# Two quarters of an edge chunk in one set of score columns: a graph-attention kernel, its first layer changed

## The chip, the cores and the metric

The kernel runs on one core of a Trainium2 chip. The metric is the device time of one execution in microseconds (us). The kernel before takes 2269.68 us, the median of three runs (2267.27 to 2270.17).

## What is computed

Two graph-attention layers over 6,250 nodes of 128 features and 106,250 directed edges, which arrive sorted by their destination (`dst`). Each edge carries 64 message features and 32 cosine features of a time difference. Each of two heads scores an edge, the scores are turned into weights by a softmax over the edges that end in one node, and the weighted values are summed per node. Between the layers stand a batch normalisation and a relu, and behind the second layer a residual and a layer norm.

```python
q = (h @ Wq + bq).reshape(n, H, C)
k = (h @ Wk + bk).reshape(n, H, C)
v = (h @ Wv + bv).reshape(n, H, C)
e = (edge_attr @ We).reshape(-1, H, C)
alpha = einsum('ehc,ehc->eh', q[dst], k[src] + e) / sqrt(C)
a = segment_softmax(alpha, dst)
out = segment_sum((v[src] + e) * a[:, :, None], dst) + h @ Ws + bs
```

All arithmetic is in 32-bit floats.

## The kernel before

**Chunks.** A preparation cuts the sorted edges into `NC` = 105 chunks. A chunk owns at most `NN` = 64 consecutive nodes and loads a window of `CE` = 1024 edges (`T` = 8 tiles of 128). A node and a head make one score row, so a chunk has 64 x 2 = 128 rows. The preparation also tests whether the edges are sorted and whether the cuts fit; it adds up what is wrong (`worst`, `bad`, `tot`) and writes a flag `oki` (L1521 to L1526). With the flag set `ordered` runs, otherwise a slower general path.

**One chunk in layer 1** (`conv(0)`). `gather` (L796) has GpSimd fetch the source node's row for 128 edges with one indirect DMA, so eight per chunk, into tile `ff`. `transfers` (L740) sends the chunk's stores and loads on SyncE's queue: two held stores, the message rows (`fedge`, one DMA of 256 KB) and the table `ftab`, which holds for each of the 128 score rows the vector that an edge is multiplied with. `encode` (L820) makes the cosine features on VectorE (DVE) and ScalarE (ACT). `turn_in` (L849) transposes features into `fft` and `fet` (edges along the free axis). `score` (L879) makes, for each half of the chunk, a 128 x 512 tile `fps` of scores with two matmuls (L887 for node features, L888 for edge features and for a code: where an edge doesn't belong to the row's node, the code adds 2^120). `lowest` (L890) takes each row's minimum, `weigh` (L898) the exponential of the negated score, which is zero where the code was added. `turn_weights` (L904) transposes the 128 x 1024 weights in eight steps into `fpt`, with edges along the partitions, and `gather_sums` (L917) adds weights times features in eight matmuls of 225 columns (L921) into `fpa`. `divide`, `finish_turn`, `apply` and `finish` make the node's output of it.

**Order.** The instructions of each engine run in the order in which the code is written. A round k of the loop at L1125 works on several chunks at once: scores of chunk k, sums of chunk k-1, output of chunk k-2, `turn_in` of chunk k+1, `encode` of chunk k+2 and gathers of chunk k+3. The gathers are paced: `tick` (L812) ties the next gather to a step of TensorE (PE) in the round, eight in a round of layer 1. Some rounds take on other work (`rest`, L1232): the tables of later nodes (L630) and, behind them, rows of the result. The last two chunks of a layer are written out by hand (`first_ends`, L1039). Layer 2 (`conv(1)`) has the same stages with edge data that layer 1 stored, and gathers eight tiles at a time without pacing (`fetch_whole`, L807).

**Weights in two passes.** A 32-bit matmul of the program appears in the profile as two MATMUL instructions, each with a weight load (LDWEIGHTS); a transpose appears as one.

Of the kernel before, what the change touches and what calls it, by code (L numbers as in the profile page):

```python
# [7 lines left out]
F32 = mybir.dt.float32  # L8
I32 = mybir.dt.int32
AF = mybir.ActivationFunctionType  # L10
OP = mybir.AluOpType
AX = mybir.AxisListType

P = 128
D = 128
H = 2
C = D // H
# [5 lines left out]
GE = GT * P  # L23
# [21 lines left out]
T = 8  # L45
# [8 lines left out]
FW = 1 + D + EC  # L54

APART = 2.0 ** 120
HIGHEST = 2.0 ** 119

LG = 10
# [604 lines left out]
def ordered(ctx: ExitStack, tc: tile.TileContext, pl, x, dst, edge_attr_64, conv2, bn_g, bn_b, out):  # L664
# [39 lines left out]
    def conv(c, extra, first_blocks=None):  # L704
# [20 lines left out]
        ends = []  # L725

        done = []

        def send(to, ap, after=None):
            dma = nc.sync.dma_start(to, ap)  # L730
# [9 lines left out]
        def transfers(k, after=None):  # L740
            for to, ap in held:
                send(to, ap, after)
                after = None
            held.clear()
            if not on(k):
                return
            s = plan(k)
            lo, hi = first(k)
            if k % LOT == 0:
                n = min(LOT, NC - k)  # L750
                lot[:] = [nc.sync.alloc_register(name=f"at{c}_{k}_{i}") for i in range(2 * n)]
                nc.sync.load(lot, pl.starts[0:1, 2 * k:2 * (k + n)])
            s.nb = nc.sync.snap(lot[2 * (k % LOT)], min_val=lo, max_val=hi)
            s.edge = load.tile([P, T * (MSG + TD)], F32, name="fedge", bufs=4)
            s.msg = s.edge[:, :T * MSG].rearrange("p (t d) -> p t d", d=MSG)
            s.z = s.edge[:, T * MSG:].rearrange("p (t d) -> p t d", d=TD)
            if c:
                send(s.edge, edge_d[k], after)
            else:
                sl = nc.sync.snap(lot[2 * (k % LOT) + 1], min_val=0, max_val=E - CE)  # L760
                send(s.msg, edge_attr_64[bass.ds(sl, CE), :].rearrange("(p t) d -> p t d", t=T), after)
            s.tab = load.tile([P, NN * H, 3 - c], F32, name="ftab")
            nc.sync.dma_start(s.tab, pl.tab_d[c][:, bass.ds(s.nb, NN)].rearrange("p n h w -> p (n h) w"))
            if c:
                s.et = ets[k % len(ets)]
                nc.sync.dma_start(s.et, et_d[k])
                s.r = load.tile([NN, D], F32, name="fr", bufs=AHEAD + 3)
                nc.sync.dma_start(s.r, res_d[bass.ds(s.nb, NN), :] if k < NC - 1 else res_d[N - NN:N, :])
# [110 lines left out]
        def score(k, u):  # L879

            s = ch[k]
            if u == 0:
                s.ps = []
            ps = p_s.tile([P, GE], F32, name="fps")
            s.ps.append(ps)
            w = slice(u * GE, (u + 1) * GE)
            tick(nc.tensor.matmul(ps, s.tab[:, :, 0], s.ft[:, w], start=True, stop=False))  # L887
            tick(nc.tensor.matmul(ps, s.tab[:EC, :, 1], s.et[:, w], start=False, stop=True), True)  # L888
# [8 lines left out]

        def weigh(k):  # L898
            s = ch[k]
            s.s = work.tile([P, CE], F32, name="fs")  # L900
            for u in range(2):
                nc.scalar.activation(s.s[:, u * GE:(u + 1) * GE], s.ps[u], AF.Exp, bias=s.bias, scale=-1.0)  # L902

        def turn_weights(k):  # L904

            s = ch[k]
            s.pt = work.tile([P, CE], F32, name="fpt")
            for u in range(2):
                pp = p_tr.tile([P, GE], F32, name="fppt", tag="tr")
                for t in range(4):  # L910
                    at = u * GE + t * P
                    turn = nc.tensor.transpose(pp[:, t * P:(t + 1) * P], s.s[:, at:at + P], ident)  # L912
                tick(turn, u == 1)
                last = nc.scalar.copy(s.pt[:, u * GE:(u + 1) * GE], pp)  # L914
            return last

        def gather_sums(k, between=None):  # L917
            s = ch[k]
            s.pa = p_a.tile([P, D + EW], F32, name="fpa")
            for t in range(T):  # L920
                add = nc.tensor.matmul(s.pa, s.pt[:, t * P:(t + 1) * P], s.f[:, t, 1:1 + D + EW], start=t == 0,  # L921
                                       stop=t == T - 1)
                if t in (1, 4, 7):
                    tick(add)
                if between and t == T // 2 - 1:
                    between()
# [401 lines left out]
def tile_gnn_resnorm(ctx: ExitStack, tc: tile.TileContext, x, src, dst, edge_attr_64, edge_weight, node_vec,  # L1328
# [13 lines left out]
    with tc.tile_pool(name="plan", bufs=1) as pl, tc.tile_pool(name="planw", bufs=2) as mw, \  # L1342
# [134 lines left out]
        def columns(t, to):  # L1477
            if t.dtype != F32:
                f = mw.tile([NC, T, P], F32, name="rowf")
                nc.vector.tensor_copy(f, t[:NC])  # L1480
                t = f
            t = t.rearrange("c t p -> c (t p)").rearrange("c (p t) -> c t p", t=T)
            for t0 in range(0, T, 4):
                pt = pp.tile([P, 4, NC], F32, name="fpx")
                for i in range(4):
                    nc.tensor.transpose(pt[:, i], t[:NC, t0 + i], ident[:NC, :NC])
                nc.vector.tensor_copy(to[:, t0:t0 + 4], pt)

        for _ in matrices(nc, got, 0, keep, bank, pl):
# [28 lines left out]
        got.tw = broadcast(nc, keep, "ftw", time_w, TD)  # L1518
        got.tb = broadcast(nc, keep, "ftb", time_b, TD)
        nc.sync.dma_start(got.wv[0], conv1["Wv"])  # L1520
        pb = pp.tile([1, 1], F32, name="pb", tag="one", bufs=1)  # L1521
        nc.tensor.matmul(pb, worst, ones[:, 0:1], start=True, stop=True)
        nc.vector.tensor_copy(bad[:, 1:2], pb)
# [43 lines left out]
```

## Time and profile before

| what | value |
|---|---|
| median of three runs | 2269.68 us |
| the profiled execution's own time | 2270.48 us |
| its span, first to last instruction | 2268.6 us |
| granted TensorE clock, mean | 0.986 |
| instructions | 38241 |
| first gather of layer 1 starts | 40.13 us |
| last gather of layer 1 starts | 1133.88 us |
| first gather of layer 2 starts | 1171.41 us |

A row of the timeline reads: start, how long the piece lasts, engine, line, operation, output <- input, shapes, count, and in brackets how long the engine had been idle and what ended that. A row of the windows reads: stretch, its length, then for each engine its busy time and, in brackets, its instructions, then the granted TensorE clock, the share of the DMA engines and GB/s. "PEld" is TensorE's weight load, "POOL" is GpSimd, "SPq" a DMA that SyncE issues. A matmul's recorded end is modelled, so the pitch of TensorE's work is read from start to start.

### The profile page before, as it was taken

How to read it: one execution, taken by the hardware profiler on the slowest of the kernel's cores; microseconds unless marked ns; L12 is line 12 of the kernel's file. 1: busy time of each engine (PE TensorE's matmuls, PEld its weight loads, DVE VectorE, ACT ScalarE, POOL GpSimd, SP SyncE). 2: the span in 40 equal slices, each digit the busy share in tenths (PEclk: the TensorE clock that was granted, in tenths of full speed). 3: DMA queues.
4: the chain of work that ended last, by engine and by line, in shares of the span. 5: the costliest groups of instructions: out<-in, count | busy, mean ns of one | idle time of the engine just before them, and what ended most of it. 6: DMA issues, size and time to landing. Idle time of an engine off the chain costs nothing.

```text
span 2268.6 us, 38241 instructions
## 1 busy us (share of the span) xinstructions
PE 2187.3 (96%) x11482; PEld 1693.3 (75%) x11482; DVE 1333.6 (59%) x4147; ACT 1349.7 (59%) x2234; POOL 1615.0 (71%) x1701
## 2 busy tenths in 40 slices
PE   5899999999999999999979999999999999999997
PEld 3688887887888878888866777777777777776775
DVE  6577777777777777777745444444444444444443
ACT  3677777777777877777743444444444444444444
POOL 3777777777777777777726777777777777777773
PEclk8999999999999999999988999999999999999999
DMA  7666666666666666666638666666666666655552
GB/s 233 182 203 180 205 209 199 184 195 198 209 192 185 209 199 212 184 201 197 187 124 227 182 186 174 173 188 181 184 181 161 192 187 175 182 169 148 164 160 57
DMA packets 208864, 417.35 MB, mean 184 GB/s; under 512 B 45216, under 2 KB 113116, under 8 KB 205324
## 3 DMA queue, kind: packets, MB, share of 16 engines
q1 hardware_dynamic: 135930, 261.60, 37.2%
q0 software_dynamic: 54144, 112.01, 20.2%
q10 hardware_dynamic: 18578, 41.21, 5.0%
q8 instruction: 97, 1.59, 0.3%
q14 instruction: 115, 0.94, 0.1%
HBM read 274.63 MB, written 140.01 MB: 183 GB/s over the span
## 4 chain that ended last, share of the span: by engine, by line
PE 84%; POOL 6%; issue 4%; DMA 3%; DVE 2%; ACT 0%; SPq 0%; DVEq 0%; ACTq 0%; POOLq 0%
PE fpa L921 25%; PE fps L887 15%; PE fps L888 14%; PE fpx L860 7%; PE fppt L912 7%; POOL ff L796 6%; PE fpg L630 4%; PE fpe L873 4%; PE fpo L977 1%; DMA ff<-hn_d,fsrcs 1%; PE fpo L970 1%; PE fpo L971 1%; PE fpo L949 1%; PE fpo L950 1%; PE fpo L978 1%
## 5 line engine op out<-in xcount | busy, mean ns | idle before, releaser
L796 POOL DMA_INDIRECT ff<-xv_d,fsrcs x840 | 808.4, 962 | 311.0 <-issue 89.6
L796 POOL DMA_INDIRECT ff<-hn_d,fsrcs x816 | 778.9, 955 | 255.8 <-issue 219.1
L921 PE MATMUL fpa<-ff,fpt 128*128 128x225 f32 x3360 | 674.4, 353 | 1.7 <-DVE ff L805 0.8
L921 PEld LDWEIGHTS fpa<-ff,fpt 128*128 128x128 f32 x3360 | 619.8, 190 | 5.4 <-issue 1.2
L868 ACT COPY fft<-fpx 128x512 f32<-128x512 f32 x412 | 241.1, 585 | 529.9 <-PE fpx L860 515.8
L894 DVE TENSOR_REDUCE flow<-fps 128x1 f32<-128x512 f32 x420 | 288.9, 689 | 408.3 <-PE fps L888 404.0
L887 PE MATMUL fps<-fft,ftab 128*128 128x512 f32 x840 | 447.0, 614 | 0.0
L914 ACT COPY fpt<-fppt 128x512 f32<-128x512 f32 x420 | 224.4, 585 | 104.3 <-PE fppt L912 99.4
L860 PE MATMUL fpx<-fident,ff 128*128 128x128 f32 x1680 | 254.3, 275 | 25.1 <-issue 15.8
L912 PEld LDWEIGHTS fppt<-fident,fs 128*128 128x128 f32 x1680 | 196.5, 141 | 109.2 <-issue 97.0
L902 ACT ACTIVATE fs<-fps,fm 128x512 f32<-128x512 f32 x420 | 266.2, 687 | 5.1 <-DVE fm L896 3.6
L860 PEld LDWEIGHTS fpx<-fident,ff 128*128 128x128 f32 x1680 | 202.8, 141 | 43.7 <-issue 28.0
L912 PE MATMUL fppt<-fident,fs 128*128 128x128 f32 x1680 | 218.8, 273 | 4.4 <-DVE fo L636 2.6
L888 PE MATMUL fps<-fxT,ftab 112*128 112x512 f32 x420 | 216.0, 595 | 0.0
L888 PE MATMUL fps<-fet,ftab 112*128 112x512 f32 x420 | 215.0, 593 | 0.0
L887 PEld LDWEIGHTS fps<-fft,ftab 128*128 128x128 f32 x840 | 164.5, 227 | 51.2 <-issue 46.5
L931 DVE TENSOR_SCALAR finv<-fpa 128x1 f32<-128x1 f32 x210 | 32.2, 153 | 235.0 <-PE fpa L921 235.0
L888 PEld LDWEIGHTS fps<-fet,ftab 112*128 112x128 f32 x420 | 105.3, 251 | 74.7 <-issue 65.4
L888 PEld LDWEIGHTS fps<-fxT,ftab 112*128 112x128 f32 x420 | 83.2, 198 | 98.5 <-issue 97.8
L902 ACT ACT_TABLE_LOAD x116 | 148.8, 1283 | 2.0
L834 DVE SCALAR_TENSOR_TENSOR farg<-fturns,farg 128x256 f32<-128x256 f32 x315 | 134.0, 425 | 10.8
L873 PE MATMUL fpe<-fident,ff 128*112 128x128 f32 x840 | 128.0, 276 | 7.6 <-DVE ff L1033 7.6
(242 smaller groups left out, 2444.7 us busy)
## 6 DMA issues: line engine op xcount, KB each, us to landing
et_d<-fet SPq DMA_DIRECT2D x105, 448.0 KB
fxT<-et_d SPq DMA_DIRECT2D x105, 448.0 KB
edge_d<-fedge SPq DMA_DIRECT2D x105, 384.0 KB
fedge<-edge_d SPq DMA_DIRECT2D x105, 384.0 KB
fedge<-in_edge_attr SPq DMA_DIRECT2D x105, 256.0 KB
ftab<-tab_d SPq DMA_DIRECT2D x105, 192.0 KB
tab_d<-fo ACTq DMA_DIRECT2D x13, 1536.0 KB
ff<-xv_d,fsrcs POOLq DMA_INDIRECT x840
```

Source lines behind the costliest of these rows:

```text
L796: row = nc.gpsimd.indirect_dma_start(out=ch[k].f[:, t, (1 if c else 0):1 + D], out_offset=None, in_=(h_d if k < RAW else hn_d) if c else p ...
L834: nc.vector.scalar_tensor_tensor(arg, turn, -part, arg, op0=OP.mult, op1=OP.add)
L860: turn = nc.tensor.transpose(px[:, t * P:(t + 1) * P], s.f[:, u * 4 + t, 1:1 + D], ident)
L868: copy(s.ft[:, u * GE:(u + 1) * GE], px)
L873: turn = nc.tensor.transpose(pe[:EC, t * P:(t + 1) * P], s.f[:, u * 4 + t, 1 + D:], ident)
L887: tick(nc.tensor.matmul(ps, s.tab[:, :, 0], s.ft[:, w], start=True, stop=False))
L888: tick(nc.tensor.matmul(ps, s.tab[:EC, :, 1], s.et[:, w], start=False, stop=True), True)
L894: nc.vector.tensor_reduce(low[:, u:u + 1], s.ps[u], AX.X, OP.min)
L902: nc.scalar.activation(s.s[:, u * GE:(u + 1) * GE], s.ps[u], AF.Exp, bias=s.bias, scale=-1.0)
L912: turn = nc.tensor.transpose(pp[:, t * P:(t + 1) * P], s.s[:, at:at + P], ident)
L914: last = nc.scalar.copy(s.pt[:, u * GE:(u + 1) * GE], pp)
L921: add = nc.tensor.matmul(s.pa, s.pt[:, t * P:(t + 1) * P], s.f[:, t, 1:1 + D + EW], start=t == 0, stop=t == T - 1)
```

## The change

The edges of a chunk are sorted by destination. In layer 1 the first 256 edges (`SE`) are now scored only against the first 32 nodes of the chunk, which are score rows 0 to 63, and the last 256 edges only against the other 32 nodes, rows 64 to 127. Both quarters share the same 256 columns of one score tile: each of their matmuls has 64 weight columns and writes 64 of the tile's 128 partitions. The middle 512 edges are scored as before. So a chunk of layer 1 has 768 score columns in the place of 1024.

- `score`: for the first tile, four matmuls of 64 weight columns by 256 edges instead of two of 128 by 512. The two of one table follow each other: rows 0 to 63, then rows 64 to 127.
- `weigh`, `lowest`, `turn_weights`: the first of two pieces has 256 columns instead of 512; six transposes instead of eight.
- `gather_sums`: for the shared columns four matmuls of 64 weight columns by 225, into the lower and the upper half of `fpa` in turn, then four of 128 by 225; eight of 128 by 225 before.
- The tiles of a chunk hold edges in another order: tiles 0 and 1 the first quarter, 2 and 3 the last, 4 to 7 the middle (`PARTS`). The message rows are loaded with three DMAs instead of one, and `columns` in the preparation follows the same order.
- The ticks stay eight a round; in `gather_sums` they stand behind the four half matmuls and behind the second and the fourth of the others.
- The preparation tests, for each chunk, that edge 255 of the window belongs to a node below the 32nd of the chunk and edge 768 to the 32nd or a later one. What fails is added to `worst`, so that the general path would be taken.
- Layer 2 keeps its code.

```diff
+SIDE = 2
+SE = SIDE * P
+ME = CE - 2 * SE
+PARTS = ((0, SE), (CE - SE, SE), (SE, ME))
...
+        spans = (slice(0, GE), slice(GE, CE)) if c else (slice(0, SE), slice(SE, SE + ME))
...
-                send(s.msg, edge_attr_64[bass.ds(sl, CE), :].rearrange("(p t) d -> p t d", t=T), after)
+                t0 = 0
+                for a, n in PARTS:
+                    send(s.msg[:, t0:t0 + n // P], edge_attr_64[bass.ds(sl + a, n), :].rearrange("(p t) d -> p t d", p=P),
+                         None if t0 else after)
+                    t0 += n // P
...
+            if c == 0 and u == 0:
+                ps = ps[:, :SE]
+                s.ps.append(ps)
+                for i, (rows, terms) in enumerate(((P, s.ft), (EC, s.et))):
+                    for v in range(2):
+                        g = slice(v * C, (v + 1) * C)
+                        add = nc.tensor.matmul(ps[g], s.tab[:rows, g, i], terms[:, v * SE:(v + 1) * SE], start=i == 0,
+                                               stop=i == 1)
+                    tick(add, i == 1)
+                return
...
-                nc.scalar.activation(s.s[:, u * GE:(u + 1) * GE], s.ps[u], AF.Exp, bias=s.bias, scale=-1.0)
+                nc.scalar.activation(s.s[:, spans[u]], s.ps[u], AF.Exp, bias=s.bias, scale=-1.0)
...
-                for t in range(4):
-                    at = u * GE + t * P
-                    turn = nc.tensor.transpose(pp[:, t * P:(t + 1) * P], s.s[:, at:at + P], ident)
+                a, b = spans[u].start, spans[u].stop
+                for at in range(a, b, P):
+                    turn = nc.tensor.transpose(pp[:, at - a:at - a + P], s.s[:, at:at + P], ident)
                 tick(turn, u == 1)
-                last = nc.scalar.copy(s.pt[:, u * GE:(u + 1) * GE], pp)
+                last = nc.scalar.copy(s.pt[:, a:b], pp[:, :b - a])
...
+            if c == 0:
+                for i in range(SIDE):
+                    for v in range(2):
+                        g = slice(v * C, (v + 1) * C)
+                        add = nc.tensor.matmul(s.pa[g], s.pt[:, i * P + v * C:i * P + (v + 1) * C],
+                                               s.f[:, i + v * SIDE, 1:1 + D + EW], start=i == 0, stop=False)
+                tick(add)
+                if between:
+                    between()
+                for t in range(2 * SIDE, T):
+                    at = (t - SIDE) * P
+                    add = nc.tensor.matmul(s.pa, s.pt[:, at:at + P], s.f[:, t, 1:1 + D + EW], start=False, stop=t == T - 1)
+                    if t in (T - 3, T - 1):
+                        tick(add)
+                return
...
+        pn = pp.tile([P, 1], F32, name="pn", tag="one", bufs=1)
+        nc.tensor.matmul(pn[:NC], ends[:, 0, :NC], ones[0:1, 0:1], start=True, stop=True)
+        begins = pl.tile([P, 1], F32, name="begins")
+        nc.vector.tensor_copy(begins[:NC], pn[:NC])
+        side = pl.tile([P, 2], F32, name="side")
+        for i, at in enumerate((SE - 1, CE - SE)):
+            nc.vector.tensor_scalar(side[:NC, i:i + 1], flats[1].rearrange("c t p -> c (t p)")[:NC, at:at + 1], begins[:NC],
+                                    NN // 2 - 0.5, op0=OP.subtract, op1=OP.is_gt)
+        nc.vector.tensor_scalar(side[:NC, 1:], side[:NC, 1:], -1.0, 1.0, op0=OP.mult, op1=OP.add)
+        for i in range(2):
+            nc.vector.tensor_add(worst[:NC], worst[:NC], side[:NC, i:i + 1])
```

On TensorE, in a round of layer 1 without other work, the order before is this, from the sums of chunk k-1 to the scores of chunk k+1 (output <- moving operand and weights or the reverse, then output shape):

```order
L921 MATMUL fpa<-ff,fpt 128x225 x8
L860 MATMUL fpx<-fident,ff 128x128 x4
L873 MATMUL fpe<-fident,ff 112x128 x4
L970 MATMUL fpo<-fat,fwv_111 128x128
L971 MATMUL fpo<-fat,fwe_85 128x128
L887 MATMUL fps<-fft,ftab 128x512
L888 MATMUL fps<-fet,ftab 128x512
L912 MATMUL fppt<-fident,fs 128x128 x8
L887 MATMUL fps<-fft,ftab 128x512
L888 MATMUL fps<-fet,ftab 128x512
```

Now the same place reads:

```order
L943 MATMUL fpa<-ff,fpt 64x225 x4
L950 MATMUL fpa<-ff,fpt 128x225 x4
L869 MATMUL fpx<-fident,ff 128x128 x4
L882 MATMUL fpe<-fident,ff 112x128 x4
L1004 MATMUL fpo<-fat,fwv_111 128x128
L1005 MATMUL fpo<-fat,fwe_85 128x128
L900 MATMUL fps<-fft,ftab 64x256 x2
L900 MATMUL fps<-fet,ftab 64x256 x2
L931 MATMUL fppt<-fident,fs 128x128 x6
L906 MATMUL fps<-fft,ftab 128x512
L907 MATMUL fps<-fet,ftab 128x512
```

Nothing has changed its place; eight matmuls of 128 weight columns stand where there were ten before, beside eight of 64 weight columns, and the transposes of weights are six. Twice in a round the engine goes from 128 weight columns to 64 and back.

On VectorE, at the end of the preparation, between the source indices and the flag, this stood before:

```order
L1487 CAST fsrcs<-fpx 128x420 x2
L1523 COPY bad<-pb 1x1
L1525 TENSOR_REDUCE tot<-bad 1x1
L1526 TENSOR_SCALAR oki<-tot 1x1
L1480 CAST rowf<-rows_185 105x1024
```

Now it is:

```order
L1522 CAST fsrcs<-fpx 128x420 x2
L1559 COPY begins<-pn 105x1
L1562 TENSOR_SCALAR side<-rows_185,begins 105x1 x2
L1564 TENSOR_SCALAR side<-side 105x1
L1566 TENSOR_TENSOR worst<-worst,side 105x1 x2
L1569 COPY bad<-pb 1x1
L1571 TENSOR_REDUCE tot<-bad 1x1
L1572 TENSOR_SCALAR oki<-tot 1x1
L1514 CAST rowf<-rows_185 105x1024
```

Six small instructions, and on TensorE one more matmul (L1557), stand ahead of the flag and of the casts of destinations and edge weights.

More of the change, by code (lines that the diff above doesn't have):

```diff
@@ L899, in weigh @@
             s = ch[k]
-            s.s = work.tile([P, CE], F32, name="fs")
+            s.s = work.tile([P, CE if c else SE + ME], F32, name="fs")
             for u in range(2):
-                nc.scalar.activation(s.s[:, u * GE:(u + 1) * GE], s.ps[u], AF.Exp, bias=s.bias, scale=-1.0)
+                nc.scalar.activation(s.s[:, spans[u]], s.ps[u], AF.Exp, bias=s.bias, scale=-1.0)
         def turn_weights(k):
             s = ch[k]
-            s.pt = work.tile([P, CE], F32, name="fpt")
+            s.pt = work.tile([P, CE if c else SE + ME], F32, name="fpt")
             for u in range(2):
                 pp = p_tr.tile([P, GE], F32, name="fppt", tag="tr")
-                for t in range(4):
-                    at = u * GE + t * P
-                    turn = nc.tensor.transpose(pp[:, t * P:(t + 1) * P], s.s[:, at:at + P], ident)
+                a, b = spans[u].start, spans[u].stop
+                for at in range(a, b, P):
+                    turn = nc.tensor.transpose(pp[:, at - a:at - a + P], s.s[:, at:at + P], ident)
                 tick(turn, u == 1)
-                last = nc.scalar.copy(s.pt[:, u * GE:(u + 1) * GE], pp)
+                last = nc.scalar.copy(s.pt[:, a:b], pp[:, :b - a])
             return last
@@ L1481, in columns @@
                 t = f
-            t = t.rearrange("c t p -> c (t p)").rearrange("c (p t) -> c t p", t=T)
+            t = t.rearrange("c t p -> c (t p)")
+            t = [t[:, a:a + n].rearrange("c (p t) -> c t p", p=P)[:NC, i] for a, n in PARTS for i in range(n // P)]
             for t0 in range(0, T, 4):
@@ L1485, in columns @@
                 for i in range(4):
-                    nc.tensor.transpose(pt[:, i], t[:NC, t0 + i], ident[:NC, :NC])
+                    nc.tensor.transpose(pt[:, i], t[t0 + i], ident[:NC, :NC])
                 nc.vector.tensor_copy(to[:, t0:t0 + 4], pt)
```

## The prediction

> **What bounds the kernel now.** I read the page's busy times first, then the gathers of layer 1 one by one, then busy time by stage, then one round of TensorE.
>
> ```profile
> PE 2187.3 (96%) x11482; PEld 1693.3 (75%) x11482; DVE 1333.6 (59%) x4147; ACT 1349.7 (59%) x2234; POOL 1615.0 (71%) x1701
> ...
> L796 POOL DMA_INDIRECT ff<-xv_d,fsrcs x840 | 808.4, 962 | 311.0 <-issue 89.6
> ```
>
> By its first line the kernel is TensorE's (PE): 96% against GpSimd's (POOL) 71%. The second line warns: 840 gathers were busy 808.4 us and idle 311.0 us before them, so layer 1 takes 1119 us of POOL, half the span. How much of the idle time can go? The timeline of POOL answers:
>
> ```profile
> 40.13 0.97 POOL L796 DMA_INDIRECT ff<-xv_d,fsrcs  x1 [24.75 <-DMA fwv<-in_L_gnn_Wv]
> 41.41 0.95 POOL L796 DMA_INDIRECT ff<-xv_d,fsrcs  x1 [0.30 <-issue]
> 42.66 0.94 POOL L796 DMA_INDIRECT ff<-xv_d,fsrcs  x1 [0.30 <-issue]
> ...
> 1133.88 0.94 POOL L796 DMA_INDIRECT ff<-xv_d,fsrcs  x1 [0.30 <-PE fppt L912]
> ```
>
> The first 16 gathers have no tick to wait for, and still start every 1.25 us with 0.30 us between them. That is POOL's own pace. Now the stages (busy us and count for PE, PEld, DVE, ACT, POOL in the first and the last two rows; the second is of the gathers alone):
>
> ```profile
> 100.00:900.00 800.00, 800.00 (x4236) 646.24 (x4235) 580.60 (x1778) 617.18 (x877) 585.27 (x608) 1.00 0.66 199
> ...
> 900.00:1100.00 200.00, 151.03 (x159) 1.00 0.67 196
> ...
> 1400.00:1600.00 200.00, 198.54 (x1052) 147.40 (x1052) 91.52 (x297) 91.77 (x192) 151.71 (x159) 1.00 0.64 182
> ...
> 2000.00:2200.00 200.00, 190.62 (x1009) 141.34 (x1008) 84.17 (x288) 93.53 (x197) 151.23 (x161) 1.00 0.57 159
> ```
>
> From 100 to 900 us there are 608 gathers, one in 800/608 = 1.316 us: PE sets the pace. From 900 to 1100 us it is 200/159 = 1.258, and in layer 2, which doesn't pace its gathers, 1.258 and 1.242: there POOL sets it. A round needs eight gathers, so POOL allows a round no shorter than 8 x 1.258 = **10.06 us**; PE's rounds between 100 and 900 us take 8 x 1.316 = 10.53 us. The change works on PE, and PE leads by 0.47 us a round only.
>
> **PE's round, and what the change takes from it.** One round without other work, by starts:
>
> ```profile
> 1135.77 0.27 PE L949 MATMUL fpo<-fident,fa 128*128 128x128 f32 x1
> ...
> 1136.87 3.21 PE L921 MATMUL fpa<-ff,fpt 128*128 128x225 f32 x16
> 1139.91 0.60 PE L860 MATMUL fpx<-fident,ff 128*128 128x128 f32 x4
> ...
> 1141.23 1.08 PE L887 MATMUL fps<-fft,ftab 128*128 128x512 f32 x2
> 1142.15 1.03 PE L888 MATMUL fps<-fet,ftab 112*128 112x512 f32 x2
> 1143.01 1.04 PE L912 MATMUL fppt<-fident,fs 128*128 128x128 f32 x8
> 1143.89 1.08 PE L887 MATMUL fps<-fft,ftab 128*128 128x512 f32 x2
> 1144.81 1.02 PE L888 MATMUL fps<-fet,ftab 112*128 112x512 f32 x2
> 1145.67 0.27 PE L949 MATMUL fpo<-fident,fa 128*128 128x128 f32 x1
> ```
>
> The round is 9.90 us, with no gap. Half a chunk's scores take 1.78 us (four instructions of 0.445), the eight transposes of weights 0.88 (0.11 each), the sums 3.04 (sixteen of 0.19).
>
> - Transposes: two fewer, **-0.22 us**. Each is a step of the row above, so this one is sure.
> - Scores of the shared tile: eight instructions of 256 columns, 0.22 each, for four of 512. One after the other they cost the old 1.78. With the two halves always side by side, 0.89. No row shows two matmuls on different halves, so these are the ends. I take a value between: if the engine keeps its order and the two passes of one matmul follow each other on their half, the second pass of the lower half can run beside the first of the upper one, and so on: five steps for eight instructions, 5 x 0.2225 = 1.11, **-0.67 us**.
> - Sums over four tiles: eight instructions of 0.19 = 1.52 before; 1.52, 0.95 or 0.76 now in the same three ways. I take 0.95, **-0.57 us**.
> - Going over to 64 weight columns and back, twice a round. Layer 2 does this once:
>
> ```profile
> 1609.20 0.60 PE L860 MATMUL fpx<-fident,ff 128*128 128x128 f32 x4
> 1609.73 0.33 PE L977 MATMUL fpo<-fwv,fat 128*64 128x64 f32 x2
> 1609.90 0.28 PE L978 MATMUL fpo<-fwe,fat 128*64 128x64 f32 x2
> 1610.02 0.28 PE L977 MATMUL fpo<-fwv,fat 128*64 128x64 f32 x2
> 1610.14 0.28 PE L978 MATMUL fpo<-fwe,fat 128*64 128x64 f32 x2
> 1610.36 1.12 PE L630 MATMUL fpg<-fhT,fm 128*128 128x512 f32 x2
> ```
>
> Four transposes take 4 x 0.11 = 0.44, so L977 comes 0.09 late; pairs of this size start 0.12 apart, so L630 comes 0.10 late. Four such steps: **+0.40 us**.
>
> Together -1.06 us a round; the ends are -1.47 (all side by side) and +0.18 (nothing side by side). A table matmul in a round adds two instructions, 0.86 as L888's two above, so the longest usual round is 9.90 + 0.86 - 1.06 = 9.70, below 10.06. So POOL takes over in every round, and it makes no difference how much of the overlap comes, as long as the saving is over 0.47.
>
> **The sum.** Stretch 100 to 900 at POOL's pace: 800 - 608 x 1.258 = 35.1 us. Bounds: at 1.25, the unpaced pitch, 40; at layer 2's mean with all its stalls, below, 29.
>
> ```profile
> L796 POOL DMA_INDIRECT ff<-hn_d,fsrcs x816 | 778.9, 955 | 255.8 <-issue 219.1
> ```
>
> (778.9 + 255.8)/816 = 1.268. Behind 900 us the gathers are at the floor already, and before 100 us too (60/48 = 1.25):
>
> ```profile
> 40.00:100.00 60.00, 45.55 (x48) 0.84 0.53 152
> ```
>
> The end of layer 1: the last gather ended at 1134.82, and PE came to `finish_turn` of chunk 101 at 1145.67, 10.85 us later, by its own backlog. Now it will wait for the gather, through `encode(104)` and `divide(101)`, which VectorE runs in this order. The timeline of POOL (first row) and the chain of waits show such a case early on:
>
> ```profile
> 78.05 0.94 POOL L796 DMA_INDIRECT ff<-xv_d,fsrcs  x1 [0.30 <-PE fppt L912]
> ...
> 79.30 5.96 DMA ff<-xv_d,fsrcs
> 85.26 0.04 DVEq L827
> ...
> 85.44 0.18 DVE frel L827
> ...
> 89.39 0.45 DVE fa L934
> ```
>
> That gather ended at 78.99, so 6.4 us to the use at 85.44; the first chunk, with emptier queues, took 1.7, from 49.85 to 51.58:
>
> ```profile
> 48.91 0.94 POOL L796 DMA_INDIRECT ff<-xv_d,fsrcs  x1 [0.30 <-issue]
> ...
> 51.58 0.17 DVE L827 TENSOR_TENSOR frel<-ff,few 128x8 f32<-128x8 f32 x1 [3.45 <-DMA ff<-xv_d,fsrcs]
> ```
>  With the middle, 4.1, and 4.4 from `frel` to the end of `fa`: 8.5, or 2.3 us less. Behind it stand a score (-0.47 with its switches), two sets of transposes (-0.44) and three sums (-0.37 each): -2.0. The tail gives 4.3 us, between 1 and 7.
>
> Nothing else: the flag comes later by six DVE instructions of about 0.15 us and one more hand-over to PE, some 1.5 us, from 31.97 to 33.5 (the hand-over of `pb`, from 30.86 to its copy's start at 31.48, took 0.62). The first gather, though, is released by a transfer that SyncE issues at 36.87 and that lands at 40.08:
>
> ```profile
> 30.86 0.19 PE L1522 MATMUL pb<-pones,worst 128*1 128x1 f32 x2
> ...
> 31.48 0.14 DVE L1523 COPY bad<-pb 1x1 f32<-1x1 f32 x1
> ...
> 31.83 0.14 DVE L1526 TENSOR_SCALAR oki<-tot 1x1 int32<-1x1 f32 x1
> ...
> 36.87 3.21 DMA fwv<-in_L_gnn_Wv
> ```
>
> So this costs nothing, and 1.5 us if that cover fails. On SyncE two more message loads stand ahead of each table load:
>
> ```profile
> 610.34 0.68 SPq L730 DMA_DIRECT2D fedge<-in_edge_attr  x1
> 616.87 0.34 SPq L763 DMA_DIRECT2D ftab<-tab_d  x1
> ```
>
> Between the two the queue idles 5.85 us, waiting for the table's buffer; two issues of 0.3 to 1.2 us fit, and a message has two rounds to land. ACT and DVE have work for 617 and 581 of 800 us, 8.1 and 7.6 a round, and lose some of it. When DVE waits for chunk k+2 in `encode`, PE can still give three ticks of the next round, so POOL holds 11 gathers, 13.8 us, against 6.4 + 4.4 for landing and DVE: it doesn't run dry.
>
> 2270.5 (the profiled execution) - 35.1 - 4.3 = **2231 us**. The median shown is 0.8 lower, so 2230 to 2231 there. The forecast's own range: 40 + 7 gives 2223; 29 + 1 - 1.5 gives 2242.
>
> **Rivals.**
> 1. *The halves don't run side by side.* Every pair in turn: +0.18 us a round, in the 608/8 = 76 rounds that PE sets: +14, at most +19 over all 105. 2284 us, slower. It decides as soon as the overlap gives less than the switches cost beyond the transposes, 0.18. For it: no row shows overlap of matmuls. Against: the two write different partitions, and even half of the overlap I assume (0.62 of 1.24, 0.44 net) brings a round within 0.03 of POOL's. Of the three ways (none, in order, full) two give my time: 0.15 for this one.
> 2. *Weight loads come out from under matmuls.* Sixteen half loads a round at 0.06, the pitch at which L977 and L978 get theirs: +0.96, net -0.10, times 76, -8: 2262 us. Against it: L921 has 16 loads in 3.04 us, each beside the matmul ahead of it. 0.05. The Trainium skill has a rule of this kind ("TensorE: Matmul & The Clock Gate", Part 3, The mechanism): a weight load overlaps running matmuls only when it goes to another row group. Both halves use all rows, so by it the loads here would be bare; L921's 0.19 us for load and matmul together, in one row group, speaks against it.
> 3. *POOL is no floor*, the ticks only pace it: then PE's 1.06 x 105 = 111 us show, 2159. The 16 unpaced gathers at 1.25 us speak against it: 0.02.
> 4. *POOL runs dry*, since smaller message pieces (512 B and 1 KB for 2 KB a partition) delay landings; half the gain, 2251: 0.04.
> 5. *The test fails* and the general path runs, slower by far: 17 edges a node put edge 255 at node 15 of 32 and edge 768 at node 45: 0.01.
>
> On rival 1 the Trainium skill ("TensorEngine Tiling (Array Packing)", Key Properties) says that tiles work independently, with weight loads and matmuls in parallel, and that a change of mode drains the engine. No run here shows the first; by it the pairs would cost 0.89 and 0.76, and the time would be the same 2231, as POOL sets it. The second agrees with the 0.10 us.
>
> **How the numbers follow.** Forecast 0.71, rivals 0.15, 0.05, 0.02, 0.04, 0.01, and 0.02 for a gain and a loss that cancel. A measurement of this kernel tells 0.2% (4.5 us) from no change. Faster: 0.71 + 0.02 + 0.04 + most of rival 2 = 0.80; same 0.04; slower 0.16. The range runs from 2220 to 2284, to take in rivals 2 and 4 and half of rival 1; the forecast's own is 2223 to 2242.
>
> **What will show it.** Gathers of layer 1 at 0.30 us idle throughout and 1.25 to 1.26 us apart between 100 and 900 us; gaps on PE in each round, with `frel` waiting for gathers; the eight instructions of the shared scores within 1.1 us; the last gather near 1099. I am wrong if PE's rounds stay above 10.06 us, or if POOL's idle time stays over 0.30 with PE as releaser.

## The result, and the profile after

| what | before | after |
|---|---|---|
| median of four runs each | 2269.24 us | 2244.56 us (2240.53 to 2246.0) |
| the profiled execution's own time | 2270.48 us | 2243.63 us |
| its span | 2268.6 us | 2241.8 us |
| first and last gather of layer 1 begin at | 40.13, 1133.88 us | 41.49, 1112.23 us |
| first gather of layer 2 begins at | 1171.41 us | 1145.28 us |

The ratio of the times is 0.9889, with a 95% interval of 0.9872 to 0.9907: 1.1% faster. The forecast was 2231 us, with 2223 to 2242 as its own range; the median lies 2.6 us above that range.

The page of the changed kernel: busy times of the engines, the chain of work that ended last by engine, and the gathers of layer 1 (busy us, mean ns of one, then idle us before them).

```profile
PE 2097.2 (94%) x11694; PEld 1522.3 (68%) x11694; DVE 1309.9 (58%) x4153; ACT 1298.6 (58%) x2234; POOL 1617.6 (72%) x1701
...
PE 74%; issue 8%; DVE 8%; DMA 6%; POOL 2%; ACT 1%; SPq 0%; DVEq 0%; ACTq 0%; POOLq 0%
...
L805 POOL DMA_INDIRECT ff<-xv_d,fsrcs x840 | 811.1, 966 | 287.0 <-issue 96.7
```

TensorE lost 90 us of busy time, and the kernel 27 us of its span. The share of TensorE in the chain fell from 84% to 74%, but POOL's did not rise: it went from 6% to 2%. What rose is VectorE (2% to 8%), DMA (3% to 6%) and "issue" (4% to 8%); that this is work which hangs on the gathers is a reading, not shown by the chain. The chain alone would not name the new bound; the timeline of POOL does:

```profile
41.49 0.96 POOL L805 DMA_INDIRECT ff<-xv_d,fsrcs  x1 [26.42 <-ACT fxT L660]
...
1112.23 0.94 POOL L805 DMA_INDIRECT ff<-xv_d,fsrcs  x1 [0.30 <-PE fpo L984]
1145.28 0.95 POOL L805 DMA_INDIRECT ff<-h_d,fsrcs  x1 [32.10 <-DVE fscale L1295]
```

Between the first and the last gather of layer 1 stand 839 pauses. Before, 128 of them were longer than 0.36 us; now 6 are (counted in the two traces). The usual pause is 0.305 us in both. Stages, as in the prediction (busy us and count of PE, PEld, DVE, ACT, POOL):

```profile
100.00:900.00 800.00, 754.22 (x4533) 537.36 (x4529) 582.01 (x1835) 596.09 (x903) 605.32 (x627) 0.99 0.67 205
900.00:1100.00 200.00, 184.08 (x1136) 135.69 (x1132) 149.44 (x466) 138.18 (x216) 151.19 (x157) 0.97 0.66 197
```

From 100 to 900 us TensorE now has 46 us without work, where it had none, and 627 gathers fit where 608 did. Who waits for whom changed with it (us in total, times, longest; the second block is the kernel before):

```profile
DVE frel L836 <- issue: 149.5, 62, 6.0
...
PE fpo L983 <- DVE fhT L1028: 56.8, 38, 4.3
...
DVE frel L836 <- DMA ff<-xv_d,fsrcs: 33.2, 11, 6.5
```

```profile
DVE frel L827 <- DMA ff<-xv_d,fsrcs: 17.1, 4, 6.5
```

`frel` is VectorE's first use of gathered rows. It waited 17.1 us for their transfers before and 33.2 now, and 149.5 more for which the profile names nothing (2.5 before). TensorE in turn waits 56.8 us for VectorE ahead of L983; ahead of the same line of the kernel before (L949) the same wait is 0.6. VectorE's waits for TensorE have shrunk (for scores from 404.0 to 282.8 us) but not gone.

One round of TensorE in the changed kernel:

```profile
598.90 0.39 PE L1005 MATMUL fpo<-fat,fwe 128*128 128x128 f32 x2
599.22 0.69 PE L900 MATMUL fps<-fft,ftab 128*64 128x256 f32 x4
599.73 0.60 PE L900 MATMUL fps<-fet,ftab 112*64 112x256 f32 x4
600.26 0.88 PE L931 MATMUL fppt<-fident,fs 128*128 128x128 f32 x6
600.98 1.09 PE L906 MATMUL fps<-fft,ftab 128*128 128x512 f32 x2
...
603.42 0.60 PE L882 MATMUL fpe<-fident,ff 128*112 128x128 f32 x4
603.95 0.98 PE L943 MATMUL fpa<-ff,fpt 128*64 128x225 f32 x8
604.86 1.79 PE L950 MATMUL fpa<-ff,fpt 128*128 128x225 f32 x8
606.48 0.60 PE L869 MATMUL fpx<-fident,ff 128*128 128x128 f32 x4
...
607.80 1.02 PE L634 MATMUL fpg<-fxT,fm 128*128 128x512 f32 x2
```

The two L1005 take 0.11 each, so the shared scores, with the change of width ahead of them, run from 599.12 to 600.26: 1.14 us for 1.78 before. The transposes take 0.72 for 0.88. The four of L882 end at 603.42 + 0.44 = 603.86, so the sums of all eight tiles take 2.62 for 3.04. The round, from 599.12 to the table work at 607.80, is 8.68 us long, where it was 9.90. (Three of the expectations below speak of 1.4 us a round; by these starts it is 1.22.)

### The profile page after: what moved, and what is told of

It reads as the page before. It is cut to its first block, busy times and chain, and to the rows that moved or that the text cites. A ratio compares the mean times of both kernels' runs of the same rounds, so it can differ in the third digit from the quotient of the medians.

```text
span 2241.8 us, 39401 instructions
## 1 busy us (share of the span) xinstructions
PE 2097.2 (94%) x11694; PEld 1522.3 (68%) x11694; DVE 1309.9 (58%) x4153; ACT 1298.6 (58%) x2234; POOL 1617.6 (72%) x1701
## 4 chain that ended last, share of the span: by engine, by line
PE 74%; issue 8%; DVE 8%; DMA 6%; POOL 2%; ACT 1%; SPq 0%; DVEq 0%; ACTq 0%; POOLq 0%
PE fpa L955 14%; PE fps L906 10%; PE fps L907 10%; PE fpx L869 7%; PE fppt L931 6%; PE fpa L950 5%; DMA ff<-xv_d,fsrcs 5%; PE fpg L634 4%; PE fpa L943 3%; PE fps L900 3%; PE fpe L882 3%; POOL ff L805 2%; DVE farg L843 2%; PE fpo L1011 2%; PE fpo L1012 1%
## 5 line engine op out<-in xcount | busy, mean ns | idle before, releaser
L805 POOL DMA_INDIRECT ff<-xv_d,fsrcs x840 | 811.1, 966 | 287.0 <-issue 96.7
L913 DVE TENSOR_REDUCE flow<-fps 128x1 f32<-128x512 f32 (+1 forms) x420 | 256.1, 622 | 287.8 <-PE fps L907 282.8
L955 PE MATMUL fpa<-ff,fpt 128*128 128x225 f32 x1680 | 337.4, 353 | 1.1 <-DVE ff L814 0.8
L906 PE MATMUL fps<-fft,ftab 128*128 128x512 f32 x630 | 335.8, 615 | 0.1
L955 PEld LDWEIGHTS fpa<-ff,fpt 128*128 128x128 f32 x1680 | 309.6, 189 | 4.0 <-ACT fft L877 1.0
L921 ACT ACTIVATE fs<-fps,fm 128x512 f32<-128x512 f32 (+1 forms) x420 | 244.2, 634 | 5.2 <-DVE fm L915 3.7
L933 ACT COPY fpt<-fppt 128x512 f32<-128x512 f32 (+1 forms) x420 | 204.0, 531 | 65.3 <-PE fppt L931 60.1
L869 PEld LDWEIGHTS fpx<-fident,ff 128*128 128x128 f32 x1680 | 202.2, 142 | 56.8 <-issue 35.1
L931 PEld LDWEIGHTS fppt<-fident,fs 128*128 128x128 f32 x1470 | 165.3, 141 | 98.8 <-issue 84.3
L931 PE MATMUL fppt<-fident,fs 128*128 128x128 f32 x1470 | 201.5, 277 | 5.5 <-ACT fo L638 3.6
L950 PE MATMUL fpa<-ff,fpt 128*128 128x225 f32 x840 | 191.4, 371 | 0.0
L950 PEld LDWEIGHTS fpa<-ff,fpt 128*128 128x128 f32 x840 | 153.6, 193 | 38.2 <-ACT fet L884 29.3
L882 PE MATMUL fpe<-fident,ff 128*112 128x128 f32 x840 | 131.5, 281 | 7.9 <-DVE ff L1067 7.3
```

What stands on the lines that cost most here:

```text
L805: row = nc.gpsimd.indirect_dma_start(out=ch[k].f[:, t, (1 if c else 0):1 + D], out_offset=None, in_=(h_d if k < RAW else hn_d) if c else p ...
L869: turn = nc.tensor.transpose(px[:, t * P:(t + 1) * P], s.f[:, u * 4 + t, 1:1 + D], ident)
L882: turn = nc.tensor.transpose(pe[:EC, t * P:(t + 1) * P], s.f[:, u * 4 + t, 1 + D:], ident)
L913: nc.vector.tensor_reduce(low[:, u:u + 1], s.ps[u], AX.X, OP.min)
L921: nc.scalar.activation(s.s[:, spans[u]], s.ps[u], AF.Exp, bias=s.bias, scale=-1.0)
L931: turn = nc.tensor.transpose(pp[:, at - a:at - a + P], s.s[:, at:at + P], ident)
```

## The experiments

Twelve runs on three chips follow. On the chip of `more_pe`, `both_layers`, `no_test` and `before_again` the kernel before took 2272.17 us, as on the first chip. On the two chips of the others it took 2622.22 and 2621.83 us: there ratios and traces can be read, and the absolute times of the expectations that assume 2270 cannot. The order below is that of the argument.

### TensorE given more work, on a chip like the first

If the gathers are the floor, TensorE can be given back half of what it saved at no cost. The six transposes of weights of a round of layer 1 are done twice, into the same place:

```diff
-                for at in range(a, b, P):
+                for at in [*range(a, b, P)] * (1 if c else 2):
                     turn = nc.tensor.transpose(pp[:, at - a:at - a + P], s.s[:, at:at + P], ident)
```

> The changed kernel with the six transposes of weights of a round of layer 1 done twice: 0.66 us of TensorE more in each of 105 rounds, and nothing else. Theory (GpSimd's gathers are the floor behind the change, with 1.4 us a round of room below them): within 6 us of the changed kernel itself, 2244 where the kernel before takes 2270 and 2627 where it takes 2620, so a ratio to the kernel before of 0.988 to 0.992 or of 1.000 to 1.005. Rival (TensorE still sets the pace): 69 us more than the changed kernel, a ratio 0.026 to 0.030 higher than its own.

It took 2242.88 us (2242.06 to 2243.89), ratio 0.9873, interval 0.9857 to 0.989. The changed kernel has 0.9889, 0.9872 to 0.9907: no difference. The page's busy times of this kernel, then one group of its TensorE timeline, then the stage from 100 to 900 us:

```profile
PE 2143.6 (96%) x12324; PEld 1588.6 (71%) x12324; DVE 1311.6 (59%) x4153; ACT 1304.7 (58%) x2234; POOL 1616.9 (72%) x1701
```

```profile
610.19 1.53 PE L931 MATMUL fppt<-fident,fs 128*128 128x128 f32 x12
```

```profile
100.00:900.00 800.00, 791.39 (x5008) 587.81 (x5009) 585.82 (x1835) 601.86 (x904) 605.82 (x629) 1.00 0.69 205
```

The extra transposes are there (twelve for six), TensorE is busy 791 of 800 us again, and 629 gathers fit in, two more than without them. So TensorE isn't the bound of layer 1 in the changed kernel, and a busy share of 96% did not make it one. The room that is left is small, 9 us in 800; without the extra work it was 46, which is 0.6 us a round and not the 1.4 of the expectation.

### The same saving in layer 2

The prediction took layer 2 to be at the gathers' pace already. Here its scores share columns too, with the same split in all four places:

```diff
...
-            if c == 0 and u == 0:
+            if u == 0:
...
-            if c == 0:
+            if True:
```

> Shared score columns in layer 2 as well, the same 1.4 us a round of TensorE less there. Theory (layer 2 is at the pace of its gathers already, 816 at 1.262 us with idle time of 0.30 us): within 6 us of the changed kernel, 2244 or 2627 as the kernel before takes 2270 or 2620. Rival (TensorE, 97 to 98 per cent busy there, is the bound of layer 2): some 100 us below the changed kernel.

2246.79 us (2241.89 to 2254.05), ratio 0.9901, interval 0.9882 to 0.9921: nothing gained. One stage of layer 2 in this kernel and, below it, in the changed one:

```profile
1400.00:1600.00 200.00, 178.94 (x1076) 117.79 (x1076) 84.90 (x301) 83.89 (x195) 151.47 (x160) 0.97 0.63 180
```

```profile
1400.00:1600.00 200.00, 196.73 (x1037) 145.72 (x1036) 89.79 (x294) 91.67 (x193) 151.47 (x160) 1.00 0.62 176
```

TensorE's busy time fell by 18 us in 200, and the same 160 gathers stand in the window. TensorE was 98% busy there and not the bound.

### What the test in the preparation costs

This kernel leaves out the change's test of the columns (`pn`, `begins`, `side`) and keeps the rest:

```diff
-        pn = pp.tile([P, 1], F32, name="pn", tag="one", bufs=1)
...
-            nc.vector.tensor_add(worst[:NC], worst[:NC], side[:NC, i:i + 1])
```

> The changed kernel without the test in the preparation (it leaves out the check of the columns, one matmul and six operations of VectorE). Theory (the test holds up everything behind the flag): the flag at 31.8 to 32.0 us and the first gather of layer 1 at 40.0 to 40.4 instead of 41.5 to 41.9. Rival (the first gather waits for a transfer, or for the scheduling of the casts, whatever the test does): the first gather stays at 41.2 to 41.9.

The kernel before ran beside it, for its trace:

> The kernel before, for its trace beside the others on this chip. Where it takes 2620: the median pitch of its gathers in layer 1 at 1.25 us as on the first chip, and over 100 stalls of one to two us in each layer, as in the changed kernel's trace of such a chip; a rival is that only the changed kernel's trace has them, and then the kernel before would be slow for another reason. Where it takes 2270: as in the profile of before, under 10 stalls in layer 2.

From the timelines: the preparation in the changed kernel, the first gather of layer 1 without the test, and that of the kernel before; last, the group of layer 1's gathers on the page of the kernel before:

```profile
31.81 0.15 DVE L1559 COPY begins<-pn 105x1 f32<-105x1 f32 x1
31.99 0.33 DVE L1562 TENSOR_SCALAR side<-rows,begins 105x1 f32<-105x1 int32 x2
...
33.42 0.14 DVE L1572 TENSOR_SCALAR oki<-tot 1x1 int32<-1x1 f32 x1
```

```profile
40.23 0.96 POOL L805 DMA_INDIRECT ff<-xv_d,fsrcs  x1 [24.94 <-DVE fbits L790]
```

```profile
40.10 0.96 POOL L796 DMA_INDIRECT ff<-xv_d,fsrcs  x1 [24.77 <-DVE fbits L781]
```

```profile
L796 POOL DMA_INDIRECT ff<-xv_d,fsrcs x840 | 809.9, 964 | 308.7 <-issue 87.2
```

Without the test the flag is back at 31.93 and the first gather at 40.23. With it, on chips of this kind, the first gather began at 41.49, 41.59 (`more_pe`) and 40.74 (`both_layers`). The test does hold up what stands behind the flag. The end did not show it: the kernel without the test took 2248.46 us in its one run. Its gathers of layer 1 had 12 long pauses with 8.2 us beyond the usual pause in them instead of 6 with 4.7, layer 2's first gather came 35.1 us behind the last of layer 1 instead of 33.1, and layer 2 took 1.5 us more. A start 1.3 us earlier is less than such differences between runs.

The last row also settles a smaller question: the kernel before has gathers of 964 ns here and 962 in its first profile, the kernels behind the change 963 to 966. Of the 4 ns by which they grew in the first pair of profiles, 2 lie between two runs of one kernel; whether the change adds the rest isn't shown. As expected for such a chip, `before_again` has few long pauses in layer 2: two.

### The halves in turn

The changed kernel issues the lower and the upper half alternately. This one issues the whole lower half first, scores and sums alike, to take the overlap away:

```diff
-                for i, (rows, terms) in enumerate(((P, s.ft), (EC, s.et))):
-                    for v in range(2):
+                for v in range(2):
+                    for i, (rows, terms) in enumerate(((P, s.ft), (EC, s.et))):
...
```

> The changed kernel with the half matmuls in another order: all of the lower half, then all of the upper half, in the scores and in the sums. Theory (halves run side by side only when they follow each other, each pair costing one step): six steps more, three of 0.22 and three of 0.19 us, so the shared scores take about 1.7 instead of 1.05 us and the shared sums 1.5 instead of 0.91; a round of TensorE with other work comes to 10.4 us, above the gathers' 10.2: 2253 to 2264 us. Rival (TensorE pairs the halves in whatever order they stand, or the time comes from the fewer transposes alone): 2240 to 2248 us.

2630.94 us beside 2622.22 of the kernel before on that chip, ratio 1.0041, interval 1.0025 to 1.0058. The time tells nothing of the overlap, for two reasons. The chip is one on which TensorE's saving is worth nothing (below). And the edit did not take the overlap away:

```profile
600.80 0.69 PE L900 MATMUL fps<-fft,ftab 128*64 128x256 f32 x4
601.31 0.61 PE L900 MATMUL fps<-fet,ftab 112*64 112x256 f32 x4
```

The engine's order in the program is now lower `fft`, lower `fet`, upper `fft`, upper `fet`, two passes each. The starts in the trace are still four pairs (us):

```
changed kernel:  599.216 599.223 | 599.518 599.522 | 599.734 599.738 | 599.954 599.958
halves in turn:  600.800 600.813 | 601.098 601.111 | 601.314 601.327 | 601.534 601.547
                 fft     fft       fft     fft       fet     fet       fet     fet
```

The second of a pair comes 13 ns behind the first instead of 4 to 7, and the steps are the same. The trace doesn't say which half a record belongs to; with the order of issue read from the code, each half of the columns works through its own matmuls, and what is issued for the upper half starts while earlier ones of the lower half still wait. That is the mechanism of the expectation's rival, pairs in whatever order the halves stand. This experiment failed at its purpose: a kernel whose halves do run one after the other was not tried.

### Order and loads of the change without the sharing

The new order of edges, the three message loads and the test stay; scores, transposes and sums are those of before:

```diff
-        spans = (slice(0, GE), slice(GE, CE)) if c else (slice(0, SE), slice(SE, SE + ME))
+        spans = (slice(0, GE), slice(GE, CE))
...
-            if c == 0 and u == 0:
+            if False:
...
```

> The kernel before with the new order of edges, the three message loads a chunk and the test in the preparation, but without shared columns. Theory (these parts cost a later first gather, 1.4 us, and gathers longer by 3 to 4 ns each, up to 3 us): 2269 to 2274 us, with the first gather near 41.5 us and a mean gather of 965 ns or more in layer 1. Rival (they cost nothing, and the later start and longer gathers of the changed kernel come from its faster pace): 2266 to 2270 us, first gather near 40.1 us or later without effect, mean gather 962 ns.

> The new order of edges, the three message loads and the preparation's test, but no sharing of score columns. Theory (the sharing alone brings the gain; loads and test cost the first gather about 1.4 us, the gathers some 4 ns each): where before takes 2270, 2270 to 2276, ratio 1.000 to 1.003, the first gather at 41.2, the gathers' mean at 962 to 966 ns. Rival (the order and the smaller loads bring part of the gain): 2262 or below. Rival (smaller loads cost what is missing of the gain, some 10 us): 2280 or above.

2629.27 and 2631.41 us, ratios 1.0031 (1.0019 to 1.0043) and 1.0032 (1.0019 to 1.0044): 0.3% slower, close to the theory's 1.000 to 1.003, though on chips where the sharing brings nothing either. The first gather began at 41.19 and 41.33 us, as late as the theory said; the gathers' mean is 962 ns in both, not the 965 or more of `loads_test`, so longer gathers didn't come from these parts here. What the loads alone do on a chip like the first was not run.

### Chips on which the kernel before takes 2622 us

The changed kernel itself ran on one of these chips:

> The changed kernel itself, beside the kernel before on one chip. Theory (GpSimd's gathers are the floor of layer 1 as soon as TensorE's round is shorter): where the kernel before takes some 2270 us, 2240 to 2248, with the gathers of layer 1 at a mean pitch of 1.276 us and under 10 stalls over 0.36 us; where it takes some 2620, because all gathers stall for another reason, TensorE's saving is hidden already, and the ratio is 0.995 to 1.005. Rival (TensorE still sets the pace, so that its 1.4 us a round show everywhere): the ratio is 0.99 or below on any chip.

2627.08 us, ratio 1.002, interval 1.001 to 1.0029, as the theory says for such a chip; the rival's 0.99 or below did not come. The gain of 1.1% is gone. The gathers of both layers in this kernel, and those of layer 1 in the second run without the sharing:

```profile
L805 POOL DMA_INDIRECT ff<-xv_d,fsrcs x840 | 803.3, 956 | 480.7 <-issue 172.4
L805 POOL DMA_INDIRECT ff<-hn_d,fsrcs x816 | 779.2, 955 | 448.8 <-issue 213.9
```

```profile
L805 POOL DMA_INDIRECT ff<-xv_d,fsrcs x840 | 807.8, 962 | 478.3 <-issue 169.6
```

A gather is no slower than on the first chip (956 ns), and its median pitch is 1.25 us there too. But the gathers of the changed kernel are idle 194 us longer in layer 1 (480.7 for 287.0) and 192 us longer in layer 2 than on the first chip; without the sharing they are idle as long here (478.3). A stretch of layer 2, where the code doesn't tie gathers to TensorE's steps, shows how:

```profile
1632.90 1.02 PE L907 MATMUL fps<-fxT,ftab 112*128 112x512 f32 x2
...
1636.95 0.69 DVE L913 TENSOR_REDUCE flow<-fps 128x1 f32<-128x512 f32 x1 [2.78 <-remote]
...
1639.92 0.58 ACT L877 COPY fft<-fpx 128x512 f32<-128x512 f32 x1 [5.25 <-remote]
1640.32 0.94 POOL L805 DMA_INDIRECT ff<-hn_d,fsrcs  x1 [2.30 <-remote]
```

VectorE picks up scores that TensorE finished at 1633.92 three microseconds later, and about once a round the gathers stop for some 2 us. The word "remote" says that the signal that ended the wait came with no instruction's end close before it. The trace does record that signal, a change of a semaphore (a counter that other engines wait for). For the three waits shown it is TensorE's own; the one for the scores came at 1636.93. In this trace 1600 of TensorE's 2347 recorded changes come over 0.1 us behind the last recorded end of a TensorE instruction that makes one, 475 of them over 1 us; in that of the first chip 2 of 2800, and VectorE's and ScalarE's come in time on both chips (2 late of 1934 and of 758 here). Of the 198 us by which the long pauses of layer 1's gathers exceed the usual pause, 195 end with TensorE's semaphore. The granted clock is not the difference: `both_layers` took 2241.89 us at 0.956, `loads_test_2` 2634.97 at 0.961.

Two more kernels took one gather in eight away. Their eighth tile holds a constant in place of gathered rows:

```diff
+                nc.vector.memset(f[:, T - 1, :1 + D], 1.0)
...
-        queue = [(k, t) for k in range(NC) for t in range(T)]
+        queue = [(k, t) for k in range(NC) for t in range(T if c else T - 1)]
...
```

> The kernel before, but with seven gathers a chunk in layer 1: the eighth tile's node features are a constant, written by VectorE; all else is computed as before. Theory (before the change TensorE set layer 1's rounds between 100 and 900 us, at 10.54 us): it stays so, and fewer gathers help only where they set the pace, at the start; 2255 to 2270 us. Rival (the gathers set layer 1's pace in both kernels): one gather less in each of 105 chunks, 1.27 us each, 133 us less: near 2136 us.

> The kernel before with seven gathers a chunk in layer 1; the eighth tile's features are a constant, TensorE's work is the same. Theory: before, TensorE set the pace of most of layer 1, so an eighth less of GpSimd's work (131 us at 1.25 us a gather) brings little: where before takes 2270, 2235 to 2270. Rival (GpSimd was the floor before the change as well): 2140 to 2160, the whole eighth.

> The changed kernel, also with seven gathers a chunk in layer 1 and a constant in the eighth tile's node features. Theory (the changed layer 1 runs at the pace of eight gathers of 1.27 us, 10.2 us a round, and TensorE alone would need some 8.53 us, 9.2 with other work): the round falls to TensorE's or to seven gathers, 8.9 us, and layer 1 loses 80 to 115 us; 2130 to 2165 us. Rival (the round now hangs on the chain from a landed gather through encode and divide back to TensorE, not on the rate of the gathers): no change beyond a few us, 2235 to 2245.

> The changed kernel with seven gathers a chunk in layer 1. Theory: behind the change GpSimd sets the pace at 10.2 us a round; seven gathers allow 8.95, and TensorE, at 8.5 to 9.3 with its table work, is close to that: where before takes 2270, 2130 to 2175, so 70 to 115 us below the changed kernel. Rival (after the change another engine or a transfer is the floor, or TensorE itself): 2225 to 2245, hardly below the changed kernel.

From the kernel before: 2492.71 and 2492.0 us, ratios 0.9518 and 0.9508 (0.9492 to 0.9524). From the changed one: 2503.14 and 2502.45, ratios 0.9558 and 0.9546 (0.953 to 0.9562).

```profile
L797 POOL DMA_INDIRECT ff<-xv_d,fsrcs x735 | 706.4, 961 | 430.4 <-issue 126.6
```

105 gathers at 1.25 us are 131 us, and 130 and 125 us went. (For the changed kernel 70 to 115 were expected, on a chip like the first.) So on these chips the gathers, with their pauses, set the pace of layer 1 in the kernel before already. For such a chip the rival of `seven_before_2` (the whole eighth) holds and the theory falls, and a TensorE that is faster by 1.2 us a round had nothing to give. Why TensorE's signals come late there stays open. With the gathers' floor taken down on a chip like the first, which these kernels were meant for, nothing was run.

## Why the prediction was right in kind and 13 us too low

The direction and the new bound came as forecast. Of the 39.4 us forecast, the profiled execution gained 26.8. Of the terms of the sum, the stretch at the gathers' pace was too large.

- **The bound.** Right. GpSimd's gathers are the floor of layer 1 behind the change. Shown by `more_pe` (TensorE has room) together with the 833 of 839 pauses at the gathers' own pace. The gathers between 100 and 900 us begin 1.277 us apart, not 1.25 to 1.26, and the last one at 1112.23 us, not near 1099. That layer 2 stood at it already is shown by `both_layers`.
- **TensorE's saving.** Forecast 1.06 us a round, measured 9.90 - 8.68 = 1.22. The scores, with the change to 64 columns, gave 0.64 and the transposes, with the change back, 0.16: 0.80 together (forecast 0.67 - 0.20 + 0.22 = 0.69). The sums gave 0.42 (0.37). (The listing of TensorE's order above has fourteen matmuls of 128 weight columns before, not ten; the sums are right.) The passes did not follow each other in five steps but in four pairs. The Trainium skill ("TensorEngine Tiling (Array Packing)", Key Properties) has tiles working independently: the pairs at 4 to 7 ns agree, and `in_turn` shows it better than the change does. As forecast, the size of this saving did not matter.
- **Rival 2, bare weight loads**, is out: the four steps of the shared sums begin 0.24, 0.19 and 0.19 us apart with their loads (603.948, 604.189, 604.379, 604.571), and an undivided sum with its load takes 0.19. The rule of the Trainium skill that stood behind the rival ("TensorE: Matmul & The Clock Gate", Part 3, The mechanism: overlap only with another row group) does not hold for these loads, which go to another half of the columns and to all rows. (The same section also lets a load into the background weight buffer run ahead, which these starts don't contradict.) Rival 1 is out by the same starts, and rival 3 (2159) by the time. Rival 4 (2251) had part of its condition: VectorE does wait longer for gathered rows. But the gathers rarely stop for it.
- **The stretch, 35.1 us: the term that was mis-sized.** The gathers between first and last became 23.0 us shorter as a whole (1093.75 to 1070.74 us), and 21.65 us at the last gather. Four parts make up the missing 13.5.
  - *The floor's pitch, 4.7 us.* I divided 200 us by 159 gathers to get 1.258. That window's count includes a gather that began ahead of it; 158 begin in it, which is 1.268 by their starts, and the stretch of 608 has the same edge. Without the count: the idle time of layer 1's gathers behind the first is 311.0 - 24.75 = 286.3 us; 839 pauses at the usual 0.305 are 255.9, so 30.4 us could go, not 35.1.
  - *Pauses that stay, 4.7 us*, in six places: idle time is 287.0 - 26.42 = 260.6 us now. Other runs had 3.8 to 8.2.
  - *Longer gathers, 2.7 us* (811.1 for 808.4 of busy time). `before_again` has 809.9 and `both_layers` 808.7, so much of it is spread between runs.
  - *The first gather, 1.4 us late.* The cover that the preparation's term named was none. The load of `fwv`, which I took for the thing waited for, moved by 0.6 us only (issued at 37.45 for 36.87). GpSimd stood, by its own wait in the trace, at the store of the last node rows, which is issued behind the flag (in the kernel before, then in the changed one):

```profile
33.91 1.91 SPq L533 DMA_DIRECT2D xv_d<-fxrest  x1
```

```profile
35.50 0.29 SPq L537 DMA_DIRECT2D xv_d<-fxrest  x1
```

That store landed at 39.19 us before and at 40.55 now, and the gather began 0.94 us behind it in both. The 1.5 us "if that cover fails" was right. `no_test` shows that the test causes it: there the store landed at 39.29.

- **The tail, 4.3 us: right, in part by luck.** Layer 2's first gather comes 26.13 us earlier, the last of layer 1 21.65: 4.5. In `both_layers` and `no_test`, whose end of layer 1 has the same code, the tail is only 2.5 and 2.4 us shorter than in the kernel before. The rows match the sum made for it:

```profile
1116.94 0.17 DVE L836 TENSOR_TENSOR frel<-ff,few 128x8 f32<-128x8 f32 x1 [3.27 <-issue]
...
1120.69 0.45 DVE L968 TENSOR_SCALAR fa<-fpa,finv 128x225 f32<-128x225 f32 x1
...
1121.73 0.30 PE L983 MATMUL fpo<-fident,fa 128*128 128x128 f32 x1 [1.10 <-DVE fhT L1028]
```

The last gather ended at 1113.17: 3.8 us to `frel` (forecast 4.1), 4.2 on to the end of `fa` (4.4), and TensorE comes to L983 after 8.6 (8.5). Layer 2 gave the last 0.7 us.

So 30.4 + 4.5 + 0.7 was to be had, and 4.7 + 2.7 + 1.4 came off: 26.8, the difference of the spans. Of what I said would show me wrong, long idle time with TensorE as releaser remains in six places of 839. The rounds do last over 10.06 us, 8 x 1.277 = 10.2, but with TensorE idle 46 us in 800: the floor I gave was too low, not TensorE too slow.

## What to carry to other kernels

Ask of a faster engine how far the next one lies behind it, in us per round; here 1.2 us were saved and 0.3 us were to be had. Take that next pace from starts, or from busy plus idle time of all its instructions: a count in a window of 200 us is off by one in 160, which was 5 us here. A gain that is only the distance to the next bound depends on that bound, and on a chip where the bound lies elsewhere it can be zero.

## What the runs showed of the hardware that was not expected

- Two 64-column halves of TensorE start 4 to 7 ns apart in the round shown when issued alternately and 13 ns apart when all of one half is issued first (medians of the scores over the layer: 7 and 13). In both, 32-bit matmuls of 256 columns follow each other at 0.22 us on each half, behind a first step of 0.30. In the second case, by the program's order, the upper half's first pass starts ahead of three passes that were issued before it.
- Going over to 64 columns takes 0.09 to 0.10 us: 599.22 instead of 599.12, and 603.95 instead of 603.86.
- One kernel before took 2269.24, 2272.17, 2621.83 and 2622.22 us in four comparisons. The difference lies in waits between engines, for the changed kernel some 190 us in each layer's gathers; a gather's own 0.96 us is the same. On the slower chips TensorE's semaphore changes up to several us behind the recorded end of its instruction (475 of 2347 over 1 us), where VectorE's and ScalarE's do not.
